# One product per chunk of a Mamba scan moved from VectorE to GpSimd

## The chip, the cores and the metric

The kernel runs on one core of a Trainium2 chip. The metric is the time of one execution on the device in microseconds (us). The engines are PE (TensorE, matrix products), DVE (VectorE), ACT (ScalarE), POOL (GpSimd) and SP (SyncE, which here issues DMAs). Each works through its own list of instructions in order and waits for the others by semaphores. SBUF is the working memory, PSUM the memory that PE writes to.

## The reference, cut to what matters

The reference is one layer of a perceiver: cross-attention, then two Mamba tracks ("fast" and "slow"), then a mixture of eight experts. There are 8 x 64 = 512 tokens of 512 features. The change lies in the Mamba part, which for each track computes

```
dt = softplus(x_dbl[..., :r] @ dtp_w.T + dtp_b)
Bm, Cm = x_dbl[..., r:r + n], x_dbl[..., r + n:]       # n = 16 states
A = -exp(A_log)
# over the 64 time steps, for each batch, channel d and state n
dA  = exp(dt_t[:, :, None] * A)
hst = dA * hst + (dt_t * u_t)[:, :, None] * B_t[:, None, :]
y   = einsum('bdn,bn->bd', hst, C_t)
# afterwards
y = (y + x * D) * silu(z)
out = y @ mout_w.T
```

There are 1024 channels in each track, and 16 states per channel. The product of the change is that of `hst` with `C_t`, before the sum over the states.

## The kernel before

Tokens lie along the free dimension (T = 512: 8 batches of 64 steps), channels along the 128 partitions. A *chunk* is 128 channels of one track, so there are 2 x 8 = 16 chunks, named (t, c). In a chunk the 16 states are taken in 8 *pairs*, n = 0, 2, ..., 14. All work of a pair is on tiles of 128 partitions by 2 x 512 columns of float32:

- ACT writes `da` (L1032), the exponential, as two instructions, into one of two PSUM tiles that alternate between pairs (`das`).
- POOL writes `db` (L1036), du times B, into one of two SBUF buffers. `du` is dt times x; the B and C rows lie, broadcast over the partitions, in tiles `bc`, loaded by SP, eight per track in nine buffers.
- DVE scans (L996): `tensor_tensor_scan` over da and db gives the states, written to the single PSUM tile `hs`.
- DVE multiplies `hs` with C into `hc` (L1005), an SBUF tile with three buffers.
- PE adds the two states of `hc` into the PSUM tile `yp` with products with the identity (L1015). In float32 each product is two instructions, so a pair has four. The first of a chunk is that of x with the diagonal of D (L1013). `yp` has one buffer.
- After the last pair, DVE multiplies `yp` with the gate `z` (L1017).

The order of the work is written out by hand: every instruction named here is kept in program order on its engine. In the turn of pair n the code issues da and db of pair n, then (`scanned`, L992) the scan and the product with C of the pair before it, then (`summed_up`, L1007) the PE products of the pair before that, and then the other work of this place (`beside`, L856). So the scan and product of pair 14 of a chunk are issued in the turn of pair 0 of the next chunk, behind the db of that pair 0; pair 14 is summed, and L1017 issued, in the turn of pair 2, behind the scan and product of pair 0.

The work beside the pairs is: dt of the next chunk, with PE (`dp`, L801), ACT (L806 to L814) and five steps on POOL (`dt_rest`, L817: L820 to L830), one behind the db of each of five pairs from pair 4; the projections, convolution and x products of the slow track during the fast one (`ix`, `cx`, `xd`); the gate `ip`, with two loads of ACT's tables in the last pair; and the output products `cp` during the slow track. At chunk (0,7) the slow track's B and C are computed and loaded, and the dt steps of chunk (1,0) come two pairs later.

After the last chunk, PE makes the rest of the output products (L1056) and the projection (L1065), and the expert stage follows, which starts by loading the weights of its first expert into memory that the Mamba stage frees.

## Time and profile before

| | us |
|---|---|
| median of 6 executions | 1348.39 (1346.75 to 1349.55) |
| the profiled execution | 1346.95 |
| its span, first to last instruction | 1345.3 |
| busy in the span: PE, DVE, ACT, POOL | 1195.1, 826.4, 572.7, 512.1 |
| scans on DVE (L996), 128 of 2.297 | 294.0 |
| products with C on DVE (L1005), 128 of 1.224 | 156.7 |
| db on POOL (L1036), 128 of 2.359 | 301.9 |
| first scan to last gate product | 419.4 to 914.8 |

The profile shows one execution. The page's slices divide the span into 40 equal parts of 33.6 us, and a digit is the busy share in tenths. Its groups read: line, engine, operation, output and inputs, shapes, count, then busy us and mean ns of one, then the idle time of the engine just before them and who ended most of it. In the timeline a row is start, duration (both us), engine, line, operation; a bracket gives the idle time before it and what ended that; "x4" is several instructions in one row. The duration of a row of several matrix products is from the first start to the last end.

### The profile page before, as it was taken

To read this page: it belongs to the slowest core of one execution; us is meant where nothing else is said; L and a number is where in the kernel's file an instruction comes from. 1 tells how busy PE (TensorE), PEld (TensorE's weight loads), DVE (VectorE), ACT (ScalarE), POOL (GpSimd) and SP (SyncE) were. 2 spreads that over 40 slices of the span, in tenths; PEclk is the share of its full clock that TensorE was granted. 3 is DMA by queue.
4 is the path that set the end of the run, shared out by engine and by line. 5 is a ranking of instruction groups with operands and counts; after the bars stand their busy time and mean duration, and the time that the engine had idled before them with its cause. 6 is when DMAs were issued, how large, how long until landed. Compare 5 with 4: busy or idle time off the path is not lost.

```text
span 1345.3 us, 14093 instructions
## 1 busy us (share of the span) xinstructions
PE 1195.1 (89%) x5030; PEld 717.8 (53%) x5030; DVE 826.4 (61%) x1226; ACT 572.7 (43%) x1152; POOL 512.1 (38%) x384
## 2 busy tenths in 40 slices
PE   4999999999966888889889988879799999999993
PEld 2444444444542333333333333324699999999982
DVE  5144443545756999999999999994423523442333
ACT  1233333333235566665655555550134523443450
POOL 4200000000025788888888888850210220122121
PEclk9999999999988999999999999999699999999987
DMA  6329900000027000100601010110791663476532
GB/s 228 131 76 300 294 1 1 0 1 0 1 79 263 16 31 1 31 16 23 268 17 31 16 47 17 55 31 0 301 351 65 253 266 117 190 286 231 197 105 82
DMA packets 95051, 148.71 MB, mean 111 GB/s; under 512 B 5968, under 2 KB 63584, under 8 KB 90864
## 3 DMA queue, kind: packets, MB, share of 16 engines
q1 hardware_dynamic: 89856, 131.31, 28.9%
q0 software_dynamic: 5104, 16.30, 3.4%
q8 instruction: 44, 0.72, 0.2%
q14 instruction: 47, 0.39, 0.1%
HBM read 122.95 MB, written 24.64 MB: 110 GB/s over the span
## 4 chain that ended last, share of the span: by engine, by line
PE 59%; DVE 28%; ACT 7%; issue 2%; DMA 2%; POOL 1%; another core or an unknown queue 0%; DVEq 0%; SPq 0%; POOLq 0%; ACTq 0%
DVE hs L996 17%; PE yp L1406 9%; PE hp L1361 9%; PE kp L393 7%; PE vp L551 6%; DVE hc L1005 6%; ACT da L1032 4%; PE yp L1015 3%; PE op L603 3%; PE sp L565 2%; PE atp L590 2%; PE ipe L237 2%; PE atp L591 2%; PE ip L852 1%; PE ap L424 1%
## 5 line engine op out<-in xcount | busy, mean ns | idle before, releaser
L1036 POOL TENSOR_TENSOR db<-du,bc 128x1024 f32<-128x1024 f32 x128 | 301.9, 2359 | 103.0 <-DVE hs L996 81.9
L996 DVE TENSOR_TENSOR_SCAN hs<-da,db 128x1024 f32<-128x1024 f32 x128 | 294.0, 2297 | 20.5 <-POOL db L1036 5.8
L1015 PE MATMUL yp<-hc,ident 128*128 128x512 f32 x512 | 248.7, 609 | 58.3 <-DVE hc L1005 57.4
L1032 ACT ACTIVATE da<-dt,an 128x504 f32<-128x504 f32 x256 | 174.9, 683 | 172.2 <-DVE hs L996 166.3
L1015 PEld LDWEIGHTS yp<-hc,ident 128*128 128x128 f32 x512 | 92.0, 190 | 202.9 <-DVE hc L1005 117.8
L1005 DVE TENSOR_TENSOR hc<-hs,bc 128x1024 f32<-128x1024 f32 x128 | 156.7, 1224 | 11.2 <-DVE hs L996 0.9
L1361 PE MATMUL hp<-xgT,w 128*128 128x192 f32 (+1 forms) x1024 | 153.8, 310 | 3.5 <-DVE xgT L1333 3.0
L1406 PE MATMUL yp<-h,w 128*128 128x192 f32 (+1 forms) x1024 | 153.0, 311 | 4.4 <-ACT h L1391 4.4
L1406 PEld LDWEIGHTS yp<-h,w 128*128 128x128 f32 x1024 | 150.4, 194 | 5.3 <-ACT h L1391 4.8
L1361 PEld LDWEIGHTS hp<-xgT,w 128*128 128x128 f32 x1024 | 149.4, 192 | 5.2 <-DVE xgT L1333 3.7
L393 PE MATMUL kp<-ctx,wk 128*128 128x400 f32 x256 | 93.6, 510 | 0.0
L383 POOL COPY qbd<-qT 32x256 f32<-32x256 f32 x32 | 12.6, 395 | 209.0 <-PE sp L565 207.7
L551 PE MATMUL vp<-wv,ctx 128*128 128x512 f32 x192 | 88.2, 604 | 0.0
L1368 ACT ACTIVATE h<-hp,ev 128x192 f32<-128x192 f32 (+1 forms) x128 | 50.9, 398 | 82.0 <-PE hp L1361 81.8
L1324 POOL DMA_DIRECT2D xg<-x_rows x11 | 6.0, 544 | 185.2 <-PE xtp L1330 175.3
L614 DVE COPY oT<-op 32x64 f32<-32x64 f32 x64 | 13.7, 214 | 93.6 <-PE op L603 93.2
L393 PEld LDWEIGHTS kp<-ctx,wk 128*128 128x128 f32 x256 | 46.3, 189 | 44.2 <-issue 14.1
L1423 DVE BATCH_NORM_STATS2 bs<-ytp 128x6 f32<-128x512 f32 (+1 forms) x13 | 8.5, 688 | 98.2 <-PE ytp L1421 98.2
L852 PE MATMUL ip<-oT,iw 128*128 128x512 f32 x128 | 60.6, 597 | 4.4 <-ACT x L910 3.4
L571 DVE CUSTOM_DVE_ANT_0 sc<-sp,madd,rsc 128x400 f32<-128x400 f32 x64 | 38.1, 629 | 38.7 <-PE sp L565 38.6
L1391 ACT ACTIVATE h<-h,ev 128x192 f32<-128x192 f32 (+1 forms) x128 | 55.9, 517 | 5.5 <-DVE h L1388 5.3
L1343 DVE TENSOR_TENSOR s<-h 128x768 f32<-128x768 f32 (+1 forms) x16 | 13.7, 857 | 70.8 <-ACT h L1368 70.8
(282 smaller groups left out, 1586.0 us busy)
## 6 DMA issues: line engine op xcount, KB each, us to landing
w<-in_w_dram SPq DMA_DIRECT2D x64, 1024.0 KB, 14.6
bc<-bcd SPq DMA_DIRECT2D x16, 1024.0 KB, 9.9
x_rows<-z SPq DMA_DIRECT2D x8, 1152.0 KB, 11.9
y_rows<-z SPq DMA_DIRECT2D x8, 1152.0 KB, 12.0
ctx<-in_ctx_dram SPq DMA_DIRECT2D x32, 200.0 KB, 3.9
iw<-in_fast_in_w_dram SPq DMA_DIRECT2D x8, 512.0 KB, 4.4
iw<-in_slow_in_w_dram SPq DMA_DIRECT2D x8, 512.0 KB, 3.7
mo<-in_slow_mout_w_dram SPq DMA_DIRECT2D x8, 512.0 KB, 4.1
```

Of the source, the lines that this page charges most:

```text
L393: nc.tensor.matmul(kp[:, :n], wk[:, k, ec * P : (ec + 1) * P], ctx_t[k][:, o : o + n], start=(k == 0), stop=(k == ND - 1),)
L551: nc.tensor.matmul(vp, ctxs[b][k][:, j * P : (j + 1) * P], wv[:, k, :], start=(k == 0), stop=(k == ND - 1))
L852: keep(nc.tensor.matmul(s[key], w[:, k, u * P : (u + 1) * P], oT[k], start=(k == 0), stop=(k == ND - 1)))
L996: keep(nc.vector.tensor_tensor_scan(hs.rearrange("p n s -> p (n s)"), q["da"].rearrange("p n s -> p (n s)"), q["db"].rearrange("p n s -> p ...
L1005: keep(nc.vector.tensor_tensor(q["hc"], hs, bcs[t][1][n][:, 1], ALU.mult))
L1015: keep(nc.tensor.matmul(yp[0], ident, q["hc"][:, j, :], start=False, stop=(n + j == NS - 1)))
L1032: keep(nc.scalar.activation(by_batch(da[:, j, :])[:, :, 1:], by_batch(dt)[:, :, 1:], AF.Exp, scale=an[:, t, k : k + 1]))
L1036: keep(nc.gpsimd.tensor_tensor(db, du.rearrange("p (o s) -> p o s", o=1).to_broadcast([P, 2, T]), bc[:, 0], ALU.mult))
L1361: nc.tensor.matmul(hp, st["w1"][k][:, i * P : (i + 1) * P], st["xgT"][:, k, :n], start=(k == 0), stop=(k == ND - 1),)
L1368: nc.scalar.activation(h[:, i, :], hp, AF.Relu, bias=st["ev"][:, i : i + 1])
L1391: nc.scalar.activation(h[:, i, :], h[:, i, :], AF.Identity, bias=st["ev"][:, NF + f : NF + f + 1], scale=st["ev"][:, f : f + 1],)
L1406: nc.tensor.matmul(yp, ws[i // 4][:, i % 4, m * P : (m + 1) * P], st["h"][:, i, :], start=(i == 0), stop=(i == NF - 1),)
```

## The change

In `scanned`, the tile `hc` is now taken before the scan. For the last pair of a chunk (n = 14) the scan writes its states to `hc` in SBUF instead of `hs` in PSUM, and the product with C is issued on POOL instead of DVE, reading `hc` and writing it in place. The other seven pairs are as they were. In POOL's list the new product stands where it is issued: behind the db of pair 0 of the next chunk and ahead of the db of pair 2.

```diff
                 def scanned(q):
 
                     t, c, n = q["of"]
-                    hs = pm.tile([P, 2, T], F32, tag="hs", name="hs")
+                    q["hc"] = mb2.tile([P, 2, T], F32, tag="hc", bufs=3, name="hc")
+                    q["late"] = n == NS - 2
+                    hs = q["hc"] if q["late"] else pm.tile([P, 2, T], F32, tag="hs", name="hs")
                     keep(nc.vector.tensor_tensor_scan(
...
                     ))
-                    q["hc"] = mb2.tile([P, 2, T], F32, tag="hc", bufs=3, name="hc")
-                    keep(nc.vector.tensor_tensor(q["hc"], hs, bcs[t][1][n][:, 1], ALU.mult))
+                    eng = nc.gpsimd if q["late"] else nc.vector
+                    keep(eng.tensor_tensor(q["hc"], hs, bcs[t][1][n][:, 1], ALU.mult))
```

## The prediction

> **What bounds the kernel now.** I read the page first: its slices, then its groups.

> ```profile
> DVE  5144443545756999999999999994423523442333
> ...
> POOL 4200000000025788888888888850210220122121
> ...
> L1036 POOL TENSOR_TENSOR db<-du,bc 128x1024 f32<-128x1024 f32 x128 | 301.9, 2359 | 103.0 <-DVE hs L996 81.9
> L996 DVE TENSOR_TENSOR_SCAN hs<-da,db 128x1024 f32<-128x1024 f32 x128 | 294.0, 2297 | 20.5 <-POOL db L1036 5.8
> ...
> L1005 DVE TENSOR_TENSOR hc<-hs,bc 128x1024 f32<-128x1024 f32 x128 | 156.7, 1224 | 11.2 <-DVE hs L996 0.9
> ```

> Slices 14 to 27 (about 420 to 914 us) are the scan stage. DVE is full there (9), POOL at 8. DVE does one scan and one product per pair, 128 of each; POOL makes db and mostly waits for DVE to free a buffer. So a DVE instruction taken away can be worth its time, but only until something else ends last. The change acts once per chunk, so I looked next at the timeline of one chunk boundary. Here (0,5) ends and (0,6) begins:

> ```profile
> 603.18 2.30 DVE L996 TENSOR_TENSOR_SCAN hs<-da,db 128x1024 f32<-128x1024 f32 x1
> 603.44 1.38 ACT L1032 ACTIVATE da<-dt,an 128x504 f32<-128x504 f32 x2
> ...
> 605.02 1.12 PE L801 MATMUL dp<-xdb,dtw 64*128 64x512 f32 x2
> ...
> 605.56 2.36 POOL L1036 TENSOR_TENSOR db<-du,bc 128x1024 f32<-128x1024 f32 x1 [1.33 <-DVE hs L996]
> 605.59 1.22 DVE L1005 TENSOR_TENSOR hc<-hs,bc 128x1024 f32<-128x1024 f32 x1
> ...
> 606.87 1.98 PE L1015 MATMUL yp<-hc,ident 128*128 128x512 f32 x4 [0.72 <-DVE hc L1005]
> 606.94 2.30 DVE L996 TENSOR_TENSOR_SCAN hs<-da,db 128x1024 f32<-128x1024 f32 x1
> ...
> 609.34 1.22 DVE L1005 TENSOR_TENSOR hc<-hs,bc 128x1024 f32<-128x1024 f32 x1
> ...
> 610.49 0.68 DVE L1017 TENSOR_TENSOR x<-yp,z 128x512 f32<-128x512 f32 x1
> ...
> 611.08 2.29 DVE L996 TENSOR_TENSOR_SCAN hs<-da,db 128x1024 f32<-128x1024 f32 x1
> ```

> Columns are start and duration. From the scan of pair 14 (603.18) DVE runs hc of 14, scan and hc of pair 0, the gate product L1017, and the scan of pair 2 at 611.08: 7.90 us. Of the 15 boundaries 13 take 7.89 to 7.91, two take 8.24 and 8.25. L1017 comes after hc of pair 0 in DVE's order, but what it needs is yp with pair 14 added: PE has that at 608.85 (606.87 + 1.98), 1.64 us before it is asked for. This slack is what the change will use up. Last, the end of the stage:

> ```profile
> 908.30 2.30 DVE L996 TENSOR_TENSOR_SCAN hs<-da,db 128x1024 f32<-128x1024 f32 x1
> ...
> 910.70 1.23 DVE L1005 TENSOR_TENSOR hc<-hs,bc 128x1024 f32<-128x1024 f32 x1
> ...
> 911.99 1.98 PE L1015 MATMUL yp<-hc,ident 128*128 128x512 f32 x4 [1.77 <-DVE hc L1005]
> ...
> 914.08 0.69 DVE L1017 TENSOR_TENSOR x<-yp,z 128x512 f32<-128x512 f32 x1 [2.15 <-PE yp L1015]
> ```

> There nothing lies beside the last hc: PE waits 1.77 us for it and then works without a gap.

> **The change, part by part.** Removed from DVE: 16 products of 1.22 us. At a boundary DVE goes from scan 14 straight to scan 0; before, that took 3.76 us (603.18 to 606.94), now about 2.30, so DVE alone would save 1.46.

> Added to POOL: 16 products of 1024 columns. No row shows this one. db is the same operation on the same sizes at 2.36; the 512-column products on POOL (L822 to L830) take 1.27, twice which is 2.54; back to back, POOL started its next db after 2.31. I take 2.36, with 2.31 and 2.54 as ends.

> [...]

> Scan 14 now writes SBUF. No row has a scan that does. DVE products of 512 columns took 0.69 with SBUF alone (L830 at 412.94) and 0.68 with a PSUM input (L1017), so I take 2.30, unchanged, and keep from -0.05 to +0.11, the latter the gap that DVE leaves after a scan (605.48 to 605.59). Scan 14 also takes over the wait for a free hc buffer; that buffer was read by PE three pairs earlier, some 7 us before, so nothing.

> The new chain. Hand-overs from rows: scan end to POOL 0.08 (605.48 to 605.56); product to PE 0.06 on DVE's (606.81 to 606.87); from POOL only one is seen, the first db to the first scan, 0.03 (419.41 to 419.44). I take 0.06, ends 0.03 and 0.15. PE to L1017 0.11 (913.97 to 914.08). L1017 to the next scan 0.59. So scan 14 to scan 2 is 2.30 + 0.08 + 2.36 + 0.06 + 1.98 + 0.11 + 0.59 = 7.48 us, and it beats 7.90 by 0.42. The other arms are shorter: DVE would reach L1017 at 2.30 + 2.40 + 1.15 = 5.85 after the start of scan 14, the chain lets it at 6.89, so DVE idles 1.04. ACT has da of pair 0 at 604.82, before scan 14 ends.

> What queues behind the waiting POOL instruction: db of pair 2. Both wait for scan 14; now the db starts at 607.92 and ends at 610.28, with its scan due at 610.66. That is 0.38 to spare. Later dbs: POOL does the five dt steps (1.93 and four of 1.27) between pairs 4 and 12. Laid end to end, db of pair 6 ends at 610.28 + 2.36 + 1.93 + 2.36 = 616.93 for a scan at 618.0, and the 1.1 us of margin does not shrink up to pair 14; POOL's busy time in the stretch 603.18 to 633.49 grows from 25.7 to 28.0 of 30.3 us. PE's queue: between dp (done 606.14) and the yp products nothing is waiting at most boundaries; the ix or cp products behind them start some 1.1 us later in the trace's time (606.87 to 607.98), and ACT's copy of ix by a few tenths, where ACT waits for DVE 0.7 to 2.3 us per pair anyway. SP's queue: no transfer moves; the bc tile that is released later is not loaded again in time to matter (eight tiles are reloaded from nine buffers, this one is the last).

> Three places differ. At (0,6) PE has eight x products (L276) ahead of yp and yp starts at 638.66 either way: gain 0.04. At (0,7) POOL is late with the db of (1,0): it is free for the product at 667.10, so L1017 comes at 667.10 + 2.36 + 0.06 + 1.98 + 0.11 = 671.61, against 671.08: loss 0.53. At the end, PE starts at 910.60 + 0.08 + 2.36 + 0.06 = 913.10 against 911.99: loss 1.11, and the expert stage, whose weight loads are issued at 941.58 after the last pp products, moves with it.

> Sum: 13 x 0.42 + 0.04 - 0.53 - 1.11 = 3.86 us faster. The profiled execution took 1346.95 (span 1345.3, 1.65 around it), so 1343.1; against the median of 1348.39 that is 1344.5.

> **Rivals.** A: the hand-over and the scan are at their dear ends. All the dear ends together (2.54, 0.15, +0.11) give 0.42 - 0.18 - 0.09 - 0.11 = 0.04 per boundary; the product alone at 2.54 gives 0.24, or 1.5 us in all. The cheap ends give 0.55, or 5.6 us. So the likeliest case spans 1342.8 to 1349.5, and the middle of its dear half, 1347, cannot be told from no change.

> B, slower: writing the scan to SBUF makes it collide with POOL's db of the next pair, which runs 601.87 to 604.23, while scan 14 should start at 603.18. Held until then it loses 1.05 per boundary: 13 x (0.42 - 1.05) - 1.6 = -9.8, so 1358.2. It decides from a delay of 0.30, where 13 x 0.12 - 1.6 is nothing. Against it: hc on DVE reads one operand from SBUF and writes SBUF, and at 605.59 it ran beside a db from 605.56, 1.22 and 2.36 as everywhere. [...]

> C: the lag on POOL, PE and ACT is not absorbed but returns within the chunk, at a db or at the ix copy. Each tenth costs 1.5 us; 0.26 per boundary wipes out the gain: 1348.4. For it: POOL is left 2.3 us in 30.3. Against: no db is within 1.1 us of being late except that of pair 2.

> D: DVE's whole saving arrives, 15 x 1.46 less 1.1: 1327.6. Against it: the L1017 chain, which nothing shortens.

> **How the numbers follow.** The likeliest case (with A) 0.68, B and any slower cousin of it 0.15, C 0.14, D 0.03. About 0.2%, 2.7 us, is what can be told from no change: faster means under 1345.7. Of the likeliest case 0.52 lies there, with D 0.55. Its remaining 0.16 and C make 0.30 the same. Slower 0.15. The range goes from 1341.5 (the cheap ends, and a little for the two long boundaries, which may shrink by 0.35 each) to 1352.0 (the mild half of B).

> **What would show it.** L996 in two forms of about equal duration; 112 products on DVE and 16 on POOL near 2.36; L1017 waiting for PE about 1 us at most boundaries, at 6.9 after the start of scan 14; boundaries of 7.5; the last yp about 1.1 later after its scan. Wrong if scan 14 starts late or runs past 2.4, if PE starts over 0.15 after POOL's product, or if scans after pair 2 wait for db or da.

## The result

| | us |
|---|---|
| predicted | 1344.5 (1341.5 to 1352.0) |
| before, 39 runs | 1348.98 |
| changed kernel, 18 runs | 1354.74 |
| ratio to before | 1.0037, 95% interval 1.0027 to 1.0047 |
| profiled execution, span | 1354.06, 1352.3 |

The change makes the kernel slower by 0.4%; a gain of 0.3% was forecast. The page of the changed kernel, slices and groups:

```profile
DVE  5144443545856988988898988983423423443333
...
POOL 4200000000025898989889998960210221122120
...
L1017 PE MATMUL yp<-hc,ident 128*128 128x512 f32 x512 | 262.1, 638 | 58.8 <-DVE hc L1007 32.8
L998 DVE TENSOR_TENSOR_SCAN hs<-da,db 128x1024 f32<-128x1024 f32 x112 | 256.8, 2293 | 17.8 <-POOL db L1038 7.4
...
L1007 DVE TENSOR_TENSOR hc<-hs,bc 128x1024 f32<-128x1024 f32 x112 | 137.1, 1224 | 8.8
```

DVE is no longer full in every slice of the scan stage (8 among the 9s), and POOL is busier. The product with C on DVE fell from 128 to 112. PE's mean for a yp product rose from 609 to 638 ns, though the edit does not touch these 512 products. The boundary from (0,5) to (0,6), in the timeline, shows where:

```profile
604.46 2.28 DVE L998 TENSOR_TENSOR_SCAN hc<-da,db 128x1024 f32<-128x1024 f32 x1
...
606.51 1.12 PE L801 MATMUL dp<-xdb,dtw 64*128 64x512 f32 x2
606.82 2.35 POOL L1007 TENSOR_TENSOR hc<-hc,bc 128x1024 f32<-128x1024 f32 x1 [1.10 <-DVE hc L998]
606.85 2.30 DVE L998 TENSOR_TENSOR_SCAN hs<-da,db 128x1024 f32<-128x1024 f32 x1
...
609.22 3.46 PE L1017 MATMUL yp<-hc,ident 128*128 128x512 f32 x4 [1.59 <-POOL hc L1007]
...
612.72 0.69 DVE L1019 TENSOR_TENSOR x<-yp,z 128x512 f32<-128x512 f32 x1 [2.25 <-PE yp L1017]
613.33 2.29 DVE L998 TENSOR_TENSOR_SCAN hs<-da,db 128x1024 f32<-128x1024 f32 x1
```

Scan 14 starts at 604.46, POOL's product ends at 609.17, and PE starts 0.05 later: this far the chain is the one that was worked out. But the four yp products take 3.46 us instead of 1.98, so the gate product (now L1019) waits until 612.72 and the boundary is 8.87 us long. At the boundary that begins at 544.00 the same instructions, with the same gap before them, took 1.98, and it is 7.39 us long:

```profile
548.76 1.98 PE L1017 MATMUL yp<-hc,ident 128*128 128x512 f32 x4 [1.58 <-POOL hc L1007]
...
550.78 0.69 DVE L1019 TENSOR_TENSOR x<-yp,z 128x512 f32<-128x512 f32 x1 [0.98 <-PE yp L1017]
551.39 2.29 DVE L998 TENSOR_TENSOR_SCAN hs<-da,db 128x1024 f32<-128x1024 f32 x1
```

The granted clock tells the two apart. Here are two stretches of the slow boundary, PE's gap and the products behind it (the columns are stretch, length, busy time of the five engines, then the granted clock, the DMA share and GB/s):

```profile
607.63:609.20 1.57, 0.00 (x1) 0.00 (x0) 1.51 (x1) 1.57 (x3) 1.57 (x2) 1.00 0.24 37
609.20:612.70 3.50, 3.48 (x5) 1.53 (x6) 1.23 (x1) 2.69 (x5) 3.50 (x2) 0.55 0.18 59
```

Behind the gap PE was granted 0.55 of its clock, as a mean over this stretch. In the timeline of weight loads this is seen as loads of 0.34 us instead of 0.19; there are 4 such loads in the scan stage before the change and 51 after it. Of the 13 ordinary boundaries (all but (0,6) and (0,7)) 8 are slow (8.70 to 9.07 us), 5 are at 7.38 or 7.39. The kernel before had one such place too, at its first boundary, which the prediction passed over:

```profile
449.10:451.20 2.10, 0.03 (x1) 0.00 (x0) 2.00 (x2) 2.09 (x4) 1.18 (x1) 1.00 0.00 0
451.20:454.90 3.70, 3.65 (x5) 1.12 (x5) 3.49 (x2) 3.18 (x6) 2.38 (x2) 0.54 0.00 0
```

From the start of the first scan to the start of the last gate product the stage took 494.6 us before and 499.4 after, 4.7 more. The other 2.3 us of the span lie ahead of it (1.0) and behind it (1.3) and were not looked into.

### The profile page after: what moved, and what is told of

Its sections match the earlier page's. It is cut to its first block, busy times and chain, and to the rows that moved or that the text cites. A ratio compares the mean times of both kernels' runs of the same rounds, so it can differ in the third digit from the quotient of the medians.

```text
span 1352.3 us, 14078 instructions
## 1 busy us (share of the span) xinstructions
PE 1205.7 (89%) x5030; PEld 724.4 (54%) x5030; DVE 805.3 (60%) x1210; ACT 570.8 (42%) x1152; POOL 547.5 (40%) x400
## 4 chain that ended last, share of the span: by engine, by line
PE 58%; DVE 24%; POOL 5%; ACT 5%; issue 3%; DMA 2%; another core or an unknown queue 0%; SPq 0%; DVEq 0%; POOLq 0%; ACTq 0%
DVE hs L998 14%; PE yp L1408 9%; PE hp L1363 9%; PE kp L393 7%; PE vp L551 6%; PE yp L1017 5%; DVE hc L1007 4%; ACT da L1034 3%; PE op L603 3%; POOL hc L1007 2%; PE sp L565 2%; DVE hc L998 2%; PE atp L590 2%; PE ipe L237 2%; PE atp L591 2%
## 5 line engine op out<-in xcount | busy, mean ns | idle before, releaser
L1017 PE MATMUL yp<-hc,ident 128*128 128x512 f32 x512 | 262.1, 638 | 58.8 <-DVE hc L1007 32.8
L998 DVE TENSOR_TENSOR_SCAN hs<-da,db 128x1024 f32<-128x1024 f32 x112 | 256.8, 2293 | 17.8 <-POOL db L1038 7.4
L1017 PEld LDWEIGHTS yp<-hc,ident 128*128 128x128 f32 x512 | 96.8, 198 | 204.0 <-issue 100.5
L1007 DVE TENSOR_TENSOR hc<-hs,bc 128x1024 f32<-128x1024 f32 x112 | 137.1, 1224 | 8.8
L1370 ACT ACTIVATE h<-hp,ev 128x192 f32<-128x192 f32 (+1 forms) x128 | 50.8, 397 | 81.9 <-PE hp L1363 81.7
L551 PEld LDWEIGHTS vp<-wv,ctx 128*128 128x128 f32 x192 | 34.7, 189 | 40.1 <-issue 39.2
```

The lines of the kernel that those rows point to most:

```text
L551: nc.tensor.matmul(vp, ctxs[b][k][:, j * P : (j + 1) * P], wv[:, k, :], start=(k == 0), stop=(k == ND - 1))
L998: keep(nc.vector.tensor_tensor_scan(hs.rearrange("p n s -> p (n s)"), q["da"].rearrange("p n s -> p (n s)"), q["db"].rearrange("p n s -> p ...
L1007: keep(eng.tensor_tensor(q["hc"], hs, bcs[t][1][n][:, 1], ALU.mult))
L1017: keep(nc.tensor.matmul(yp[0], ident, q["hc"][:, j, :], start=False, stop=(n + j == NS - 1)))
L1370: nc.scalar.activation(h[:, i, :], hp, AF.Relu, bias=st["ev"][:, i : i + 1])
```

## The experiments

Two explanations stood against each other. The clock theory: PE idles longer ahead of the products of pair 14 and is then granted less of its clock. Its rival: what POOL now does beside PE slows PE. An edit is against the changed kernel, except where the kernel before is named.

**The changed kernel once more.** No edit.

> The changed kernel once more, unaltered. Clock theory: the boundaries fall again into two groups, about 7.4 us (PE's four yp products in 1.98 us) and 8.7 to 9.1 us (the same four in up to 3.6 us, with weight loads of 0.34 instead of 0.19 us), but not the same boundaries as in the first profile are slow, since the instruction lists are the same and only the phase of the clock control differs. Rival, SBUF or semaphore traffic from POOL slows PE: the same boundaries are slow again, as the same instructions meet.

1354.34 us in one execution, beside 1348.22 for the kernel before. Slow boundaries in the first profile: chunks 1, 2, 4, 5, 9, 11, 12, 14 in order, and (0,7); in this one 1, 2, 4, 5, 9, 10, 12, 14, and (0,7). So one differs (10 for 11), the others repeat. That the same instructions can be slow or not is shown; the repeat is closer than the clock theory had it, and alone it rules out neither theory.

**The scan to SBUF, the product left on DVE.**

```diff
-                    eng = nc.gpsimd if q["late"] else nc.vector
+                    eng = nc.vector
```

> One part of the change alone: the scan of pair 14 writes SBUF, its product stays on DVE. If writing the scan to SBUF costs nothing: scan 2.28 as in the changed kernel, boundaries 7.9, time that of before (1349) within 0.2%. If the SBUF scan is to blame for the loss: boundaries 8.7 or more and 1354 or so.

1338.88 us, ratio 0.9940 (0.9918 to 0.9962): neither expectation. The half of the change that was costed at nothing is the better half by itself. The timeline of the boundary from (0,5):

```profile
600.38 1.23 DVE L1007 TENSOR_TENSOR hc<-hs,bc 128x1024 f32<-128x1024 f32 x1
...
601.52 2.28 DVE L998 TENSOR_TENSOR_SCAN hc<-da,db 128x1024 f32<-128x1024 f32 x1
...
603.84 1.23 DVE L1007 TENSOR_TENSOR hc<-hc,bc 128x1024 f32<-128x1024 f32 x1
...
603.88 5.83 POOL L1038 TENSOR_TENSOR db<-du,bc 128x1024 f32<-128x1024 f32 x2 [1.11 <-DVE hc L998]
604.98 2.29 DVE L998 TENSOR_TENSOR_SCAN hs<-da,db 128x1024 f32<-128x1024 f32 x1
```

A scan starts 1.14 us after the start of the product before it, where the two do not share `hs`; before the change it was 1.35, where the scan overwrites the `hs` that the product reads. That it waits there for the product is the likely reason; a second `hs` tile in PSUM, which would show it apart from the move to SBUF, was not tried. The gain comes twice, at scan 14 and at scan 0, and the product follows its scan 0.04 instead of 0.11 after its end. A chunk is 29.78 us instead of 30.30.

The price is on POOL: two db in 5.83 us instead of 4.66 (609.12 in the changed kernel). The first of them starts 0.04 us behind DVE's product, which takes its usual 1.23; with 2.36 for the second, the first took about 3.5 by subtraction. At (0,7), where a db had started first, it is DVE's product that takes longer, 2.53 instead of 1.23:

```profile
662.83 8.08 POOL L1038 TENSOR_TENSOR db<-du,bc 128x1024 f32<-128x1024 f32 x3
663.73 2.53 DVE L1007 TENSOR_TENSOR hc<-hc,bc 128x1024 f32<-128x1024 f32 x1
```

Before the change, DVE's product with one input in PSUM and a db that started 0.03 ahead of it took 1.22 and 2.36 side by side (605.59 and 605.56). What the longer times come from is not shown beyond that.

**One extra PE product ahead of dp**, which fills part of the gap; dp overwrites its result.

```diff
                     dp = bank("dp")
+                    for _ in range(1):
+                        keep(nc.tensor.matmul(dp, ident, oT[0], start=True, stop=True))
```

> The changed kernel with one extra product (identity with the normalised tokens) ahead of each dp, into the bank that dp then overwrites: 0.86 us more of PE work in the gap of 1.59 us ahead of the yp products of pair 14, so the gap is about 0.73 as in the kernel before. Clock theory: the yp products take 1.98 us at all boundaries that have a dp in front; boundaries 7.4 to 7.5; seven slow ones of about 1.5 us and that of (0,7) go, so 1354.7 - 12 = 1343, say 1342 to 1346, about 0.3% under before. Rival, POOL's traffic slows PE: nothing changes, or it is slower by what the extra products take, 1354 to 1356.

1341.09 us, ratio 0.9947 (0.9933 to 0.9961). More work on PE made the changed kernel about 13 us faster. Timeline of the same boundary:

```profile
603.12 1.02 PE L802 MATMUL dp<-oT,ident 128*128 128x512 f32 x2
...
604.07 1.12 PE L803 MATMUL dp<-xdb,dtw 64*128 64x512 f32 x2
...
605.92 1.98 PE L1019 MATMUL yp<-hc,ident 128*128 128x512 f32 x4 [0.73 <-POOL hc L1009]
```

With a gap of 0.73 the products take 1.98, and 12 of the 13 ordinary boundaries are 7.38 to 7.40 us; only the first is slow. POOL's product and its hand-overs are the same as in the changed kernel, so POOL's traffic is not what slowed PE. (0,7) stays slow (11.3): PE waits 2.97 there.

**The kernel before, with dp one pair later.**

```diff
-                            at(0, lambda: s.update(dp=dt_product(*nxt)))
+                            at(1, lambda: s.update(dp=dt_product(*nxt)))
```

> The kernel before, POOL untouched, with the dp product moved one pair later, behind the yp products of pair 14: PE's gap ahead of these grows from 0.73 to about 1.85 us. Clock theory: slow weight loads (0.34 us) appear at some of the boundaries, as in the changed kernel, and the four yp products there take 2.4 to 3.6 us; the time changes little (0 to 3 us more), because 1.64 us of slack lie between these products and L1017. Rival, POOL's traffic: no slow loads after the first chunk, time as before.

1352.26 us, ratio 1.0028 (1.0016 to 1.0041), and slow products came at two boundaries only. PE's gap ahead of pair 14's products grew as meant:

```profile
611.16 1.98 PE L1015 MATMUL yp<-hc,ident 128*128 128x512 f32 x4 [1.77 <-DVE hc L1005]
```

At the ten boundaries with gaps of 1.77 to 1.78 the products stayed at 1.98 or 1.99; at (0,4) they took 3.25 behind a gap of 2.13, and at (1,0) 3.68 behind 2.12. The boundaries stayed at 7.9 but for three (8.25 to 8.38), and the time went elsewhere: dt comes later (POOL's first dt step waits 22.9 us in all for ACT, 1.0 before the change). So a gap alone does not explain the changed kernel, where 1.59 was enough. What differs is the instruction ahead of the gap: there it is dp, on 64 rows of the array, here a yp product on 128.

**The extra product on 64 rows.**

```diff
-                        keep(nc.tensor.matmul(dp, ident, oT[0], start=True, stop=True))
+                        keep(nc.tensor.matmul(dp, ident[:R, :], oT[0][:R, :], start=True, stop=True))
```

> As the run with one extra product ahead of each dp, but the extra product uses 64 of the 128 rows, like dp itself; PE's busy time and its gap (0.73 us) are the same. If the clock control goes by whether PE is busy: as that run, fast boundaries of 7.4, 1341 to 1343. If it goes by how much of the array works, a product on 64 rows counts for less: gap and half-filled products together are again 2.7 us ahead of the yp products of pair 14, as in the changed kernel, and slow weight loads come back at a good part of the boundaries; 1346 to 1354.

1339.96 us, ratio 0.9937 (0.9917 to 0.9956), boundaries as in the run with 128 rows (12 ordinary ones at 7.39 or 7.40, the first 8.24). With the half-filled product ahead of dp, too, the products behind the gap stayed fast at these 12.

**dp itself on 128 rows.** The 64 added rows of weights are zero; dp is the same.

```diff
-                dtws[t] = mbr.tile([R, DI], F32, tag="dtw", name=f"dtw{t}")
-                later(nc.sync.dma_start(dtws[t], a[f"{TR[t]}_dtp_w"]))
+                dtws[t] = mbr.tile([P, DI], F32, tag="dtw", name=f"dtw{t}")
+                nc.gpsimd.memset(dtws[t][R:], 0.0)
+                later(nc.sync.dma_start(dtws[t][:R], a[f"{TR[t]}_dtp_w"]))
...
-                xdbs[t] = mbr.tile([R + 2 * NS, T], F32, tag="xdb", name=f"xdb{t}")
-                nc.scalar.copy(xdbs[t], xd[: R + 2 * NS, :])
+                xdbs[t] = mbr.tile([P, T], F32, tag="xdb", name=f"xdb{t}")
+                nc.gpsimd.memset(xdbs[t][R + 2 * NS :], 0.0)
+                nc.scalar.copy(xdbs[t][: R + 2 * NS], xd[: R + 2 * NS, :])
...
-                    keep(nc.tensor.matmul(dp, dtws[t][:, c * P : (c + 1) * P], xdbs[t][:R, :], start=True, stop=True))
+                    keep(nc.tensor.matmul(dp, dtws[t][:, c * P : (c + 1) * P], xdbs[t], start=True, stop=True))
```

> The changed kernel with dp made on all 128 rows of the array instead of 64: the added 64 rows of weights are zero, so dp is the same, its duration (1.12 us) too, and PE's gap behind it stays 1.59 us. Theory: the clock control counts how full the array is, and the half-filled dp ahead of the gap counts as partly idle (in the kernel before and in the run with dp moved, gaps of 1.78 us behind full products were never followed by slow loads; in the changed kernel gaps of 1.59 behind dp were, 8 times of 13). Then the slow boundaries go: 7.4 everywhere but at (0,6), (0,7) and perhaps (1,6), 1341 to 1345. Rival, only PE's gaps count: 7 to 9 slow boundaries as in the changed kernel, 1352 to 1356.

1340.94 us, ratio 0.9944 (0.9927 to 0.9960): about 13 us less than the changed kernel, from rows of zeros. Timeline, and the same two stretches:

```profile
601.92 1.02 PE L803 MATMUL dp<-xdb,dtw 128*128 128x512 f32 x2
...
604.72 1.98 PE L1019 MATMUL yp<-hc,ident 128*128 128x512 f32 x4 [1.78 <-POOL hc L1009]
```

```profile
602.80:604.70 1.90, 0.14 (x1) 0.00 (x0) 1.79 (x2) 1.87 (x4) 1.90 (x2) 1.00 0.27 37
604.70:608.20 3.50, 3.48 (x8) 1.63 (x9) 2.52 (x3) 2.69 (x5) 3.38 (x3) 1.00 0.15 55
```

dp starts 0.09 sooner after scan 14 and takes 1.02 instead of 1.12, so the gap is longer, 1.78 us, and yet the clock stays at 1.00 and all 13 ordinary boundaries are at 7.39 or 7.40, the one without dp, (1,6), too. (In the changed kernel the long boundaries, 8.70 us and more, were 7 of the 11 ordinary ones with a dp and then a gap of 1.58 or 1.59, and (1,6), behind a gap of 2.63; the first boundary has no gap.)

**Another pair on POOL.** Pair 2, product issued one turn later, db with three buffers, bc with eight.

```diff
-                    q["late"] = n == NS - 2
+                    q["late"] = n == 2
...
-                    eng = nc.gpsimd if q["late"] else nc.vector
-                    keep(eng.tensor_tensor(q["hc"], hs, bcs[t][1][n][:, 1], ALU.mult))
+                    if not q["late"]:
+                        keep(nc.vector.tensor_tensor(q["hc"], hs, bcs[t][1][n][:, 1], ALU.mult))
+
+                def on_pool(q):
+                    t, c, n = q["of"]
+                    keep(nc.gpsimd.tensor_tensor(q["hc"], q["hc"], bcs[t][1][n][:, 1], ALU.mult))
...
+                            if len(behind) > 2 and behind[-3]["late"]:
+                                on_pool(behind[-3])
```

> The same move for another pair: pair 2 of each chunk goes through SBUF and POOL instead of pair 14; POOL's product is issued one turn later, behind the next db; db gets a third buffer, bc eight instead of nine. Nothing but the sum yp waits for it then, so POOL's and PE's latency should not show. If the boundary chain to L1017 was the whole cause of the small gain: chunks of 28.5 to 29 us (POOL's 28.0 of work is close to it), 1322 to 1332. If moving work to POOL slows things wherever it is done: 1345 or more.

1347.09 us, ratio 0.9986 (0.9971 to 1.0002): no gain, but no loss either, so neither expectation holds as it was meant. In the list of waits POOL's first dt step now waits for ACT, 37.8 us in all, and in the groups the scans wait for POOL's db:

```profile
POOL u L820 <- ACT e L812: 37.8, 13, 3.4
```

```profile
L998 DVE TENSOR_TENSOR_SCAN hs<-da,db 128x1024 f32<-128x1024 f32 x112 | 257.0, 2294 | 40.1 <-POOL db L1042 17.5
```

Freed from the gate product, the move seems to be held by the circle of POOL, ACT and DVE around dt and db. That is read from the waits alone; which link is the first was not followed, and the run also changes the buffers of db and bc.

**Two scans to SBUF, and the version without (0,7).** Products on DVE, pairs 12 and 14; in the second kernel all pairs of chunk (0,7) are as before.

```diff
-                    q["late"] = n == NS - 2
+                    q["late"] = n >= NS - 4 and (t, c) != (0, NCH - 1)
```

> Scans of the last two pairs of a chunk (12 and 14) write SBUF, all products stay on DVE. If the gain of the run with pair 14 alone (1338.9 against 1348.2, a chunk 29.78 instead of 30.30) is that DVE no longer waits between a product and the next scan for the one hs tile: another 0.5 us per chunk, about 1331. If it was peculiar to pair 14: 1339. If the products with two SBUF inputs hold up POOL (db 3.5 instead of 2.36 us next to each) so far that a db is late: 1340 or more.

> Scans of pairs 12 and 14 into SBUF with their products on DVE, except in chunk (0,7), where POOL is late and the product of pair 14 had to wait for POOL's db (boundary 10.0 instead of 7.9 us). That boundary returns to 7.9, so about 2 us under the run with both pairs everywhere (1337.3): 1335. If the wait at that boundary had another cause: 1337.

1337.33 us, ratio 0.9923 (0.9894 to 0.9951), a chunk 29.48: pair 12 brings 0.30, not 0.5, since the earlier start of scan 14 was gained already. Without (0,7), 1335.88, ratio 0.9908 (0.9888 to 0.9928); that boundary returned from 10.0 to 7.89, but the two intervals overlap, with four executions each. The cause of the 10.0 was not quite the expected one: there the product of pair 14 took 1.32 us, and it was the scan of pair 0 that waited 2.24 us for POOL's db. The last kernel has the lowest median of all.

## Why the prediction was wrong

Term by term in us, from the two traces. A boundary is taken as the change in the time from its scan 14 to the next chunk's, and the end as that from the last scan to the start of the last gate product.

| term of the sum | predicted | measured |
|---|---|---|
| 13 ordinary boundaries | -5.46 | +1.64 (5 fast: -4.33; 8 slow: +5.97) |
| (0,6) | -0.04 | -0.19 |
| (0,7) | +0.53 | +2.43 |
| end of the stage | +1.11 | +1.06 |
| chunk (0,0) | 0 | -0.20 |
| sum | -3.86 | +4.74 |

- **What failed: PE's 1.98 us in the new chain.** It was taken from a row where PE had waited 0.72 us, and used where it waits 1.59 behind the half-filled dp. The sum put no price on that wait. At 8 of the 13 ordinary boundaries PE was then granted half of its clock for about 3.4 us, and the products took up to 3.67. At a slow boundary this costs about 1.5 us (a chunk of 31.1 instead of 29.58), on the one path that the change had just made the longest. The price is shown by the runs with an extra product and with dp on 128 rows: 0.9947 and 0.9944 of the kernel before, where the changed kernel is at 1.0037.
- **The chain itself was right.** Without the clock it is 7.39 us (7.48 predicted), L1019 at 6.78 (6.89) with DVE waiting 0.98 (1.04). POOL's product took 2.35 (2.36), the hand-over to PE 0.05 (0.06).
- **Scan 14 to SBUF "unchanged" was too dear**, in the safe direction: it runs 2.28, starts 0.21 sooner, and the fast chunks gain 0.72 instead of 0.42. The gap of 0.13 after DVE's product (606.81 to 606.94), likely a wait for the one `hs` tile, was in the trace and was not read as a wait.
- **(0,7)** was predicted late by the right mechanism (POOL behind), at a quarter of the cost: PE idles 2.95 us there and its products take 3.78.
- **The end** was right in this execution, from 5.78 to 6.84, by luck: PE waited 2.63 us there and still had its full clock. In the repeat the same products took 3.42 and the end 8.29.
- **The rivals.** B, the collision of scan and db, fell: scan 14 ran beside a db in 2.28. C, a backlog on POOL, PE or ACT within the chunk, is not what happened. B's sign (slower) came true, from a cause that was not listed.
- **A slip in the range:** the case of a product of 2.54 was worked out for the 13 ordinary boundaries alone. At (0,7) and at the end it costs 0.18 more each, so 1.2 us are left of the gain and not 1.5. Nothing hangs on it.
- **What would have shown it:** the prediction saw that nothing waits in PE's queue ahead of pair 14, and took it as harmless. The page's PEclk row, the first boundary at 451.25 (3.59 for the four products behind a gap of 2.1) and the 0.54 in that stretch were there to be read.

The clock records of the traces say more about which boundaries turn slow. In the traces of the two kernels the granted clock changes, within the scan stage, only at points that lie whole multiples of 3.413 us apart (3 points before the change, 25 after it). In the changed kernel it falls to 0.50 at, among others, 486.70, 517.42, 578.86 and 609.58 us (9, 18 and 9 steps apart), and comes back one or two steps later. So take PE's work step by step of this grid. The first three rows are of the changed kernel: the step ahead of a fall, the step behind it, and the step that holds most of the gap at the fast boundary. The last two are of the run with dp on 128 rows, at its boundary (0,1):

```profile
606.17:609.58 3.41, 1.82 (x4) 0.59 (x4) 3.20 (x3) 3.37 (x6) 2.77 (x2) 1.00 0.18 36
609.58:612.99 3.41, 3.41 (x5) 1.35 (x4) 1.16 (x2) 2.31 (x4) 3.41 (x2) 0.50 0.11 41
544.73:548.14 3.41, 2.44 (x6) 0.62 (x4) 3.41 (x2) 2.94 (x5) 2.30 (x2) 1.00 0.01 3
```

```profile
483.83:487.24 3.41, 1.63 (x4) 0.49 (x3) 3.31 (x3) 3.23 (x6) 3.25 (x2) 1.00 0.00 0
487.24:490.65 3.41, 3.41 (x9) 1.52 (x8) 2.43 (x3) 1.85 (x3) 3.41 (x2) 1.00 0.00 0
```

PE was busy 1.82 us in the step ahead of the fall, over 1 us of it with dp on 64 rows; in the run with dp on 128 rows a step with 1.63 us kept the clock at 1.00. The scan stages of the two kernels have 13 steps ahead of a fall and 264 other steps at full clock. If time on 64 rows counts 0.4, the 13 hold at most 1.35 us of work and the 264 at least 1.57. If it counts in full, the 13 hold up to 2.00, and no bound leaves fewer than 7 on the wrong side. The 0.4 is an estimate fitted to these two traces (0.2 and 0.6 part the steps as well) and may not hold elsewhere. By this reading the same gap is slow at one boundary and harmless at the next by where the grid falls on it: with a gap of 1.59 or 1.58 the step held 1.82 us at the slow boundary above and 2.44 at the fast one.

The gap alone does not sort the boundaries. Gaps of 1.58 or 1.59 us behind a product on half of the rows came with slow products at 7 of 11 boundaries of the changed kernel, and gaps of 2.12 and 2.13 behind full products at two boundaries of the run with dp moved; gaps of 1.77 or 1.78 behind full products did so at none of ten there, nor at an ordinary boundary of the run with dp on 128 rows.

What stays open: how products on other numbers of rows count, how the granted clock is set, and why pair 2 gains nothing, which is explained only as far as its waits.

## What to carry to other kernels

When work moves off the bound engine, look at what its consumers do while they wait: here a PE that idled 1.59 us instead of 0.72 came back at 0.50 of its clock at 7 of 11 boundaries, and then its products (up to 3.67 us instead of 1.98), not the moved work, set the end. Giving PE more to do there, an extra product that is overwritten or rows of zeros, turned the loss into a gain (0.9947 and 0.9944 of the kernel before, where the changed kernel is at 1.0037). And try each half of a change alone: here the tile that was only a means (the scan to SBUF) gave the gain by itself (1338.88), and the move of the product added nothing to it even where the clock held (1340.94).
